# Softmax sums folded across partitions by transfers in a four-layer graph network on one Trainium2 core

## The chip, the cores and the metric

The kernel runs on one core of a Trainium2 chip. The core has a matrix engine (TensorE, PE in the profile, with its weight loads as PEld), VectorE (DVE), ScalarE (ACT), GpSimd (POOL), and a queue engine (SyncE, SP) that issues transfers; POOL issues transfers too. Matrix products are written to PSUM, which has eight banks; everything else is worked on in SBUF, with 128 partitions. The metric is the device time of one execution in microseconds; the time before is the median of three, 2737.14 us (2736.57 to 2737.26).

## The reference

Sixty-four graphs of 256 nodes with 256 features pass four layers; each layer's result is added to its input and normalized. The first is a masked attention with eight heads of 32 features and a feed-forward part, the second and third are graph attention layers, the fourth is a relational convolution in two steps. The change touches the first layer alone:

```python
qkv = x @ Wqkv.T + bqkv                       # 8 heads of 32
scores = einsum('bhqd,bhkd->bhqk', q * scale, k)
scores = where(allowed[:, None], scores, -inf)   # edge, edge back, or diagonal
attn = softmax(scores, axis=-1)
ctx = einsum('bhqk,bhkd->bhqd', attn, v)
x = layernorm(x + ctx @ Wo.T + bo, ln1_g, ln1_b)
ff = relu(x @ W1.T + b1) @ W2.T + b2
x = layernorm(x + ff, ln2_g, ln2_b)
```

## The kernel before

Each graph is recorded as a list of operations (`graph(g)`): engine, cost, what it reads and writes, and a function that issues it. A planner (`Plan.schedule`) then goes through the operations of all 64 graphs at once and writes one order for each engine. It takes operations by due date, `DUE[kind] + LATER[graph]`, two tables in the file, as soon as their inputs, their buffers (rings of a set size, `RINGS` and `SMALL`) and their engine are free by the planner's own costs; for PE it also weighs a change of tile shape against the due date (`WORTH`, `HOLD`), and `WINDOW` says how far an operation may go ahead of the earliest one that waits. So the order is written out by hand in effect, graphs overlap deeply, and a change of one operation can move all others.

Keys lie on partitions and queries along the free dimension. In `attention`, for each of two blocks of 128 keys (kt), eight scores products are made in row tiles of 32 x 128 (L969; the mode is called "row"); r counts the four heads of a row tile, hg the two halves of the heads. ACT takes the exponential (L975), DVE multiplies by the mask (L977), which gives eight tiles p of [128 keys, 2 hg, 256 queries]. DVE adds the two key blocks into four tiles `both` (L982). Then `values` issues, as one operation of PE in column tiles of 128 x 32 (mode "col"): for each half hg four products of a matrix of ones with `both` (L991), which spread the sum over 128 keys to 32 partitions for each head, and eight products of v with p (L996). Each half has a bank: sums in its second part, values in its first. DVE takes the reciprocal of the sums straight from PSUM, 128 x 256 for each half (L1002), and multiplies (L1003). ACT adds the inverse up for a check that picks a general path for unusual inputs (L1005).

`product_plus` then multiplies by Wo and adds the residual. In `feed_forward` DVE multiplies the normalized x1 by ln1_g and adds the row b2 (which was added to ln1_b in the set-up), both by `with_row` (L782). `add_row_later` and `add_later` (L787) make such an addition by a transfer instead: POOL issues a transfer that adds its source to its destination; bo, ln2_b and the residual of the last layer are added so. `masks` turns the adjacency by four PE transposes (L911) and makes the masks. `layer_norm` has statistics on DVE, the inverse root in four small POOL instructions (L887 to L890) and the scaling on ACT (L894). The full products go through `product` (L873), the gathers of the convolution are L1155. Transposed inputs of the layers go through DRAM by two SP transfers (rows, T).

Of the kernel before, what the change touches and what calls it, by code (L numbers as in the profile page):

```python
# [18 lines left out]
P = 128  # L19
# [14 lines left out]
RINGS = {"x": 3, "adj": 4, "bits": 2, "am": 2, "gm": 6, "T": 4, "qk": 2, "v": 2, "p": 12, "both": 4, "inv": 1, "ctxT": 2, "X": 8,  # L34
         "xr": 1, "hid": 1, "h": 3, "e": 3, "n": 1, "rel": 3, "hi": 2, "lo": 2, "o": 4, "blocks": 1, "turned": 1, "xT": 2, "cols": 2, "pf": 3}
DRAM = {"rows": 8, "row": 6}
SMALL = {"mv": 8, "st": 4, "rstd": 8, "r": 6, "rdeg": 4}


WORTH, HOLD, WAIT, LOCK = 20.0, 0.0, 1000000.0, -0.5  # L40
WINDOW, FIRST, TAIL = 4.0, 6, 58
LANES = 8
DUE = [
    115.11, 130.1, 87.27, 113.55, 184.78, 267.91, 127.15, 3.7, 6.4, 850.28, 907.96, 17.01, 767.99, 288.87, 535.33, 276.68, 323.52, 314.8, 295.86, 329.82,
    300.15, 372.49, 286.87, 287.98, -502.68, 591.19, 64, 190.54, 194.31, 213.9, 713.3, 602.04, 241.89, 284.25, 282.43, 286.42, 332.5, 286.53, 340.1, 391.1,
    -896.08, 82.57, 223.73, 1512.3, 652.66, -43.08, 40.01, 326.22, 390.1, 385.75, 460.35, 501.93, 1085.72, 819.32, 729.09, 1434.36, 1462.97, 1572.86, 309.27, 377.7,
    422.98, 298.61, 489.54, 349.1, 349.77, 403.91, 409.77, 1039.63, 1164.93, 1206.11, 1047.88, 1793.82, 1345.99, 941.63, 462.04, -143.68, -426.28, -563.2, -305.02, 262.4,
    -8.54, -682.53, -1425.23, -878.48, -910.48, 17.76, -1230.15, -1241.9, -450.83, -995.94, -1138.75, -609.23, -940.48, -121.13, -36.53, 517.96, -269.05, 397.54, 54.48, 413,
    377.06, 153.19, 158.68, -378.26, 790.96, -31.03, 404.99, 300.98, 1238.57, 734.43, 1000.75, 626.51, 101.96, 382.13, 45.13, 270.56, -211.2, 112.91, -26.02, 715.95,
    909.95, 879.4, 1800.2, 738.61, -248.98, -17.6, 171.18, 86.17, 653.43, -436.69, 887.7, -60.25, 1415.03, -622.37, 760.39, 726.88, -39.87, 361.21, 51.78, -354.13,  # L50
    -811.15, -996.74, -21.07, -458.08, -355, -638.8, -301.25, -345.83, 35.99, -729.94, 342.61, 978.89, 501.93, 624.52, -156.62, 34.99, -355.8, -535.26, -1056.55, -853.61,
    -309.82, -604.29, -123.96, -430.91, 250.59, -935.54, -71.5, 785.28, 299.06, 741.23, 514.78, 1612.86, 44.41, -201.89, -507.28, 48.76, -1134.8, -1513.38, -738.99, -2121.1,
    -1887.25, -2427.69, -1547.71, -1074.55, -1743.55, -801.23, -1039.08, -1445.41, -1451.37, -1811.92, -1599.65, -1352.15, -803.41, 105.4, 51.2, -2.45, 905.11, 340.42, 479.09, 446.27,
    -346.11, -241.48, -1320.8, -1184.67, 227.95, -410.93, 181.58, 411.97, 33.28, 533.62, 973.02, 416.68, 625.02, -116.64, 219.42, -238.55, -103.18, 369.86, -1126.9, -254.14,
    -62.97, -478.61, -760.52, 195.37, 133.89, -1164.69, -221.19, 309.39, -223.51, -1384.43, -912.86, -586.25, -502.37, -752.61, -194.22, -177.7, -903.8, -82.98, 212.44, 450.15,
    -20.63, 600.03, 718.67, -372.99, -463.15, -655.56, -114.2, -441.38, -98.81, -1186.92, 2.55, 33.89, -212.9, 343.42, -941.93, -141.06, 434.71, -230.33, -762.23, -500.28,
    -737.15, -1236.95, 350.32, -429.54, 392.55, 735.93, -165.46, 17.17, -406.76, -280.33, -545.61, -118.67, -562.59, -662.05, -637.17, -123.17, -299.09, -894.99, -728.14, 308.8,
    -407.46, -591.06, -1279.97, -1171.47, -1185.92, -532.14, -839.14, -1199.67, -1382.19, -1710.49, -1500.13, -823.47, -1317.15, -1651.44, -1534.52, -1542.11, -1999.83, -2099.36, -2677.74, -1674.04,
    -2031.11, -886.93, -741.03, 141.07, -201.09, -665.49, -899.61, -1034.61, -519.13, 753.8, -330.91, 224.95, -439.11, -74.6, -388.8, 150.07, 320.46, 266.34, 661.45, -131.11,
    -575.29, -614.71, -909.95, -860.38, -218.26, -502.7, 299.21, -466.82, -157.72, -96.09, 95.71, -751.12, -80.72, -711.21, -1440.05, -1626.75, -1496.54, -701.82, -2131.37, -1553.57,  # L60
    -767.95, -883.9, -451.78, -721.17, -77.66, -81.75, -876.87, -264.16, -284.81, 164.33, 500.84, 572.97, 751.67, 221.66, -573.04, -421.79, -309.92, 661.24, -78.37, 822.6,
    402.49, 814.87, 925.8, 120.82, 1121.82, 521.23, 871.11, 987.71, 661.55, 675.71, 250.34, -481.05, -752.44, -688.49, -790.45, -353.78, -477.33, -799.05, -598.48, -834.15,
    135.16, 359.04, -419.04, -153.16, -427.9, -63.74, 206.11, 144.64, -396.59, 87.54, -508.49, 33.99, 247.18, -231.56, 116.24, 559.54, 113.68, 945.19, 114.83, 632.95,
    846.63, 23.88, 241.92, -60.66, 167.66, 426.06, -250.81, -25.85, -886.96, 163.03, 213.44, 144.25, -197.06, 214.87, 469.41, 48.09, 314.49, 729.23, 840.48, 272.15,
    949.87, -274.06, 407.94, 518.88, 627.68, -253.81, -324.22, 788.98, 182.1, 73.25, -283.59, -278.9, -438.37, -351.07, -11.1, 234.91, 791.22, 267.52, -262.82, 221.58,
    -55.85, -273.21, -716.88, -232.74, -243.65, -337.37, -686.64, 243.63, -363.44, 102.34, -294.19, 157.49, -122.58, 818.8, 167.06, -139.62, 564.19, 183.5, 40.04, 561.24,
    -469.96, -301.06, 183.9, -432.22, 344.47, -19.44, 175.22, -329.23, 111.52, 31.67, 0, 12.49, 16.35, 40.7, 13.03, 29.97, 79.66, 87.72, 88.16, 92.57,
    16.9, 42.2, 63.91, 67.37, 69.2, 69.57, 64.77, 66.51, 67.73, 68.1, 54.65, 63.05, 66.15, 90.74, 93.34, 103.29, 93.94, 113.24, 100.44, 111.1,
    101.32, 106.37, 89.66, 91.55, 102.68, 90.95, 92.88, 92.14, 95.53, 92.74, 96.15, 112.62, 115.22, 115.84, 108.16, 120.58, 126.02, 128.08, 123.52, 127.74,
    128.55, 132.38, 133.45, 134.52, 135.25, 136.34, 139.84, 156.74, 162.92, 141.05, 141.83, 146.74, 158.73, 159.93, 153.03, 155.22, 160.92, 162.78, 158.68, 159.54,  # L70
    161.3, 162.04, 154.36, 156.09, 161.67, 162.41, 156.95, 157.81, 160.55, 163.15, 165.1, 168.73, 172.37, 173.1, 174.18, 178.53, 179.69, 180.41, 181.13, 184.82,
    188.33, 190.19, 190.97, 195.88, 202.19, 203.65, 203.07, 206.36, 222.82, 225.76, 209.06, 211.91, 217.09, 223.82, 225.27, 228.89, 231.63, 234.38, 242.79, 245.03,
    235.73, 243.83, 244.01, 246.19, 248.14, 251.65, 257.58, 258.36, 263.28, 272.62, 274.23, 269.16, 273.95, 276.54, 341.81, 276.37, 276.67, 281.05, 288.88, 287.58,
    292.81, 294.47, 301.47, 303.32, 303.53, 307.8, 309.41, 309.85, 304.06, 309.25, 311.17, 313.08, 313.83, 318.66, 320.01, 324.08, 327.59, 217.6, 300.09, 321.45,
    331.08, 331.85, 336.77, 350.16, 352.09, 353.9, 355.27, 348.44, 350.37, 351.98, 353.57, 356.31, 359.28, 360.19, 360.79, 357.08, 357.99, 359.21, 361.32, 361.85,
    365.25, 366.27, 367.05, 374.16, 388.51, 395.12, 397.74, 400.66, 385.92, 388.51, 398.17, 401.4, 402.41, 406.64, 404.62, 407.66, 408.19, 415.16, 418.79, 420.65,
    446.91, 460.58, 469.56, 476.66, -42.08, -71.22, 47.55, 3.95, 87.01, -47.02, 84.87, 96.85, 43.29, 49.34, 127.81, 93.06, 163.1, 82.32, 60.43, 233.39,
    93.62, 90.44, -0.5, 120.06, -23.99, 59.25, 35.15, -243.24, 80.37, 53.47, 200.92, -73.58, -7.08, 5.9, -5.15, 25.23, 43.87, 9.22, -39.39, -39.72,
    -111.42, -25.63, 15.17, 9.26, 110.12, -23.73, 207.1, 32.19, 46.32, 175.57, 73.87, -13.49, 97.45, -54.1, 63.07, 26.32, 36.13, -21.71, 254.66, 142.72,
    97.69, 92.02, 135.98, 306.53, 204.66, 18, 8.92, 47.55, 119.05, -168.79, 195.29, 2.68, 311.48, 151.91, 107.66, 214.4, 509.65, 39.08, 110.14, 228.99,  # L80
    218.6, 168.24, 162.95, 261, 207.45, 107.57, 85.27, 116.9, 164.82, 190.13, 200.94, 178.43, 163.52, 204.35, 300.87, 365.21, 103.17, 173.45, 85.86, 207.98,
    118.88, 159.89, 216.01, 206.38, 237.86, 161.11, 165.29, 97.74, 298.8, 356.49, 241.18, 307.97, 312.06, 315.69, 319.21, 317.42, 336.22, 140.04, 396.8, 241.36,
# [266 lines left out]
def tile_gnn_stack(ctx: ExitStack, tc: tile.TileContext, t: dict, out: bass.AP):  # L349
# [267 lines left out]
    def main_path(plan):  # L617
# [139 lines left out]
        def graph(g):  # L757
# [12 lines left out]
            def new(ring, shape, dtype=F32):  # L770
                return plan.tile(ring, shape, dtype)
# [702 lines left out]
```

## Time and profile before

| what | value |
| --- | --- |
| median of three runs | 2737.14 us |
| profiled execution, its own time | 2740.2 us |
| its span, first to last instruction | 2738.3 us |
| granted TensorE clock, mean | 0.995 |
| instructions | 48644 |
| DMA traffic | 329.91 MB, mean 120 GB/s |
| share of 16 DMA engines: hardware queue, software queue | 36.1%, 11.9% |
| transfers that add, issued by POOL | 64 bo, 64 ln2_b, 62 residuals, 256 KB each |
| their median time from issue to landing | 4.5, 3.8 and 4.6 us |

In a group's row, the text before the bar names the line, the engine, the operation, what it writes and reads, and how often; after the bar stand the busy time in all, the mean in ns of one, and the idle time of the engine before such instructions with what ended it. Matmuls are pipelined, and their ends are modelled, so a matmul's own duration is longer than its share of PE's time; distances from start to start tell that share. PE's fp32 matmuls have two records each. The chain of waits is followed back from the last instruction and shows, piece by piece, what held up the end.

### The profile page before, as it was taken

Reading aid. Unit: us, or ns where it says so; the run is one execution under the profiler, and the core shown is the slowest. Engines: PE = TensorE matmul, PEld = TensorE weight load, DVE = VectorE, ACT = ScalarE, POOL = GpSimd, SP = SyncE. Lnnn points to the kernel's source line nnn. Section 1 sums busy time; section 2 is a strip of 40 time slices with the busy share of each in tenths; the row PEclk is TensorE's granted clock in tenths of the full one; section 3 lists DMA queues with packets and bytes.
Section 4 is the critical chain, followed back from the end, with each engine's and each line's share of the span. In section 5 each row is a group of like instructions: output and inputs, shape, how many; then the busy total and the mean of one; then the engine's idle time right before and its main releaser. Section 6 shows DMA issues by size and latency. Waiting matters only on the chain.

```text
span 2738.3 us, 48644 instructions
## 1 busy us (share of the span) xinstructions
PE 2712.7 (99%) x15808; PEld 2115.7 (77%) x15808; DVE 2465.2 (90%) x6538; ACT 1598.4 (58%) x3830; POOL 935.5 (34%) x1747
## 2 busy tenths in 40 slices
PE   8999999999999999999999999999999999999997
PEld 6887877777787787777777877877877777778774
DVE  6789989999999999999999999999999999988977
ACT  4446555556556556556555565565565555655767
POOL 2233333334333333333333333343333333332222
PEclk8999999999999999999999999999999999999999
DMA  7345545454454454554544544544545546364211
GB/s 187 95 110 130 130 116 129 119 127 123 127 135 120 128 130 121 129 124 129 133 120 124 139 119 125 135 121 127 129 121 132 125 128 147 97 143 108 51 47 40
DMA packets 609611, 329.91 MB, mean 120 GB/s; under 512 B 391694, under 2 KB 600616, under 8 KB 609352
## 3 DMA queue, kind: packets, MB, share of 16 engines
q1 hardware_dynamic: 564984, 275.72, 36.1%
q0 software_dynamic: 44368, 51.01, 11.9%
q8 instruction: 128, 2.10, 0.3%
q14 instruction: 131, 1.07, 0.1%
HBM read 182.60 MB, written 94.23 MB: 101 GB/s over the span
## 4 chain that ended last, share of the span: by engine, by line
PE 97%; DVE 1%; DMA 1%; ACT 1%; issue 0%; SPq 0%; POOL 0%; POOLq 0%
PE bank L873 80%; PE bank L969 5%; PE bank L1155 4%; PE bank L996 4%; PE bank L991 2%; PE bank L911 1%; DMA wqkv<-in_WqkvT_dram 0%; PE bank L802 0%; DMA rows<-turned 0%; ACT turned L813 0%; DVE p L977 0%; ACT e L1170 0%; DMA T<-rows 0%; DVE inv L1002 0%; ACT X L894 0%
## 5 line engine op out<-in xcount | busy, mean ns | idle before, releaser
L887 POOL TENSOR_SCALAR rstd<-mv 128x2 f32<-128x2 f32 x384 | 148.7, 387 | 1415.1 <-DVE mv L884 469.0
L873 PE MATMUL bank<-cw,T 128*128 128x512 f32 x1024 | 469.0, 592 | 0.0
L873 PE MATMUL bank<-T,w 128*128 128x256 f32 x2048 | 466.6, 380 | 0.0
L873 PE MATMUL bank<-w,hid 128*128 128x256 f32 x2048 | 457.0, 381 | 0.0
L873 PEld LDWEIGHTS bank<-w,hid 128*128 128x128 f32 x2048 | 397.0, 196 | 43.0 <-issue 3.4
L873 PEld LDWEIGHTS bank<-T,w 128*128 128x128 f32 x2048 | 384.8, 190 | 53.8 <-issue 2.0
L975 ACT ACTIVATE p<-bank 128x512 f32<-128x512 f32 x512 | 298.8, 603 | 169.9 <-PE bank L969 169.7
L894 ACT ACTIVATE X<-X,rstd 128x256 f32<-128x256 f32 x640 | 350.0, 599 | 78.1 <-POOL rstd L890 77.3
L977 DVE TENSOR_TENSOR p<-p,am 128x512 f32<-128x512 f32 x512 | 336.6, 681 | 27.4 <-ACT p L975 22.8
L888 POOL TENSOR_TENSOR rstd<-rstd,neghalf 128x2 f32<-128x2 f32 x384 | 315.0, 820 | 32.0
L873 PEld LDWEIGHTS bank<-cw,T 128*128 128x128 f32 x1024 | 198.8, 195 | 164.5 <-issue 144.8
L1031 ACT ACTIVATE hid<-bank,col_b 128x256 f32<-128x256 f32 x512 | 212.5, 469 | 105.3 <-PE bank L873 104.1
L873 PE MATMUL bank<-h,e 128*128 128x259 f32 x1024 | 264.3, 382 | 0.0
L873 PE MATMUL bank<-gw,T 128*128 128x258 f32 x1024 | 255.1, 381 | 0.0
L873 PE MATMUL bank<-xT,wqkv 128*128 128x256 f32 x1024 | 253.7, 385 | 0.9 <-DVE xT L865 0.9
L1002 DVE RECIPROCAL inv<-bank 128x256 f32<-128x256 f32 x128 | 217.2, 1729 | 30.7 <-PE bank L996 30.5
L882 DVE BATCH_NORM_STATS2 st<-X 128x6 f32<-128x256 f32 x640 | 238.3, 414 | 2.2
L873 PEld LDWEIGHTS bank<-gw,T 128*128 128x128 f32 x1024 | 198.8, 196 | 46.3 <-issue 24.6
L873 PEld LDWEIGHTS bank<-h,e 128*128 128x128 f32 x1024 | 186.5, 190 | 46.4 <-issue 14.9
L873 PEld LDWEIGHTS bank<-xT,wqkv 128*128 128x128 f32 x1024 | 193.0, 192 | 30.6 <-issue 2.5
L1155 PE MATMUL bank<-hi,rel 128*128 128x258 f32 (+1 forms) x512 | 182.6, 364 | 0.1
L824 DVE STREAM_TRANSPOSE turned<-X 128x512 f32<-128x512 f32 x236 | 166.1, 704 | 4.6 <-ACT X L894 3.1
(147 smaller groups left out, 4676.9 us busy)
## 6 DMA issues: line engine op xcount, KB each, us to landing
rows<-turned SPq DMA_DIRECT2D x295, 256.0 KB
T<-rows SPq DMA_DIRECT2D x295, 256.0 KB
adj<-in_adj_dram SPq DMA_DIRECT2D x128, 256.0 KB
x<-in_x_dram SPq DMA_DIRECT2D x64, 256.0 KB
xr<-in_x_dram SPq DMA_DIRECT2D x64, 256.0 KB
x<-row_bo POOLq DMA_DIRECT2D x64, 256.0 KB, 4.5
xr<-row_ln_b POOLq DMA_DIRECT2D x64, 256.0 KB, 3.8
out_dram<-o SPq DMA_DIRECT2D x64, 256.0 KB
```

Of the source, the lines that this page charges most:

```text
L824: dve(0.63, lambda: nc.vector.transpose(turned().rearrange("p k (b n i) -> p (k b) i n", b=4, i=NB), xt().rearrange("p i (j c) -> p j i c" ...
L873: nc.tensor.matmul(dst, lhsT=lhs(c), rhs=rhs(c), start=(c == 0), stop=(c == n - 1))
L882: nc.vector.bn_stats(stat()[:, i, :], y()[:, i, :])
L887: nc.gpsimd.tensor_scalar(rstd()[:, 0, :], mv()[:, :, 1], 1.0, EPS, op0=ALU.mult, op1=ALU.add)
L888: nc.gpsimd.tensor_tensor(rstd()[:, 0, :], rstd()[:, 0, :], neghalf[:, 0:NB], op=ALU.pow)
L894: nc.scalar.activation(y()[:, i, :], y()[:, i, :], AF.Identity, bias=rstd()[:, 1, i : i + 1], scale=rstd()[:, 0, i : i + 1])
L969: nc.tensor.matmul(s[r]()[:, hg, :], lhsT=qk()[f, KB + hg, kt * P : (kt + 1) * P], rhs=qk()[f, hg, :], start=True, stop=True)
L975: act(0.58, lambda pr=pr, k=k, sr=s[r]: nc.scalar.activation(pr(), sr(), AF.Exp, accum_out=seen_sum[:, k : k + 1]), [s[r]], [pr])
L977: dve(0.60, lambda pr=pr, kt=kt: nc.vector.tensor_tensor(pr(), pr(), am()[:, kt, None, :].to_broadcast([P, KB, N]), op=ALU.mult), [pr, am] ...
L1002: dve(1.67, lambda hg=hg, pc=pc: nc.vector.reciprocal(inv()[:, hg, :], pc()[:, 1, :]), [pc], [(inv, hg)])
L1031: act(0.36, lambda f=f, k=k, ph=ph: nc.scalar.activation(hid()[:, f + k, :], ph()[:, k, :], AF.Relu, bias=b1[:, f + k : f + k + 1]), [ph, ...
L1155: nc.tensor.matmul(pa()[:, 0:n], lhsT=rel()[:, i, j * P : (j + 1) * P], rhs=part()[:, i, 0:n], start=(c == 0), stop=(c == len(terms) - 1))
```

## The change

The four tiles `both` become one tile of [128, 2, 4, 256]. After the four additions, two adding transfers from POOL fold it: for the first half of the heads, partitions 64 to 127 are added to 0 to 63, for the second, partitions 0 to 63 to 64 to 127. The products of ones then take 64 rows each and stand ahead of all products of values, eight in a row, in tiles of 64 x 32. The sums are transposed by DVE in blocks of 32 x 32, so that 16 columns hold all of them; the reciprocal is taken of those 16 columns, and a second transpose, which reads each column 32 times, spreads them again. The multiplication by the inverse then follows for both halves. ACT's sum reads the 16 columns. In `feed_forward`, b2 is added by a transfer. The rings change (adj from 4 to 3, pf from 3 to 2, both from 4 to 1 larger tile, inv to two tiles `sums`, a small ring `compact`), as do `WORTH`, `HOLD`, `WINDOW` and all of the tables `DUE` and `LATER`; LATER steps by 41.772 before and by 41.415 after in its middle part.

```diff
-RINGS = {"x": 3, "adj": 4, "bits": 2, "am": 2, "gm": 6, "T": 4, "qk": 2, "v": 2, "p": 12, "both": 4, "inv": 1, "ctxT": 2, "X": 8,
-         "xr": 1, "hid": 1, "h": 3, "e": 3, "n": 1, "rel": 3, "hi": 2, "lo": 2, "o": 4, "blocks": 1, "turned": 1, "xT": 2, "cols": 2, "pf": 3}
+RINGS = {"x": 3, "adj": 3, "bits": 2, "am": 2, "gm": 6, "T": 4, "qk": 2, "v": 2, "p": 12, "both": 1, "sums": 2, "ctxT": 2, "X": 8,
+         "xr": 1, "hid": 1, "h": 3, "e": 3, "n": 1, "rel": 3, "hi": 2, "lo": 2, "o": 4, "blocks": 1, "turned": 1, "xT": 2, "cols": 2, "pf": 2}
-SMALL = {"mv": 8, "st": 4, "rstd": 8, "r": 6, "rdeg": 4}
-WORTH, HOLD, WAIT, LOCK = 20.0, 0.0, 1000000.0, -0.5
-WINDOW, FIRST, TAIL = 4.0, 6, 58
+SMALL = {"compact": 3, "mv": 8, "st": 4, "rstd": 8, "r": 6, "rdeg": 4}
+WORTH, HOLD, WAIT, LOCK = 18.33, 0.32, 1000000.0, -0.5
+WINDOW, FIRST, TAIL = 17.79, 6, 58
...
-                both = [new("both", [P, KB, N]) for r in range(4)]
+                both, half = new("both", [P, KB, 4, N]), P // 2
                 for r in range(4):
-                    dve(0.60, lambda r=r: nc.vector.tensor_tensor(both[r](), p[0, r](), p[1, r](), op=ALU.add),
-                        [p[0, r], p[1, r]], [both[r]], "uses")
-                inv = new("inv", [P, KB, N])
+                    dve(0.60, lambda r=r: nc.vector.tensor_tensor(both()[:, :, r, :], p[0, r](), p[1, r](), op=ALU.add),
+                        [p[0, r], p[1, r]], [(both, r)], "uses")
+                for hg in range(KB):
+                    into, out_of = slice(half * hg, half * hg + half), slice(half - half * hg, P - half * hg)
+                    op("POOL", 1.3, lambda hg=hg, into=into, out_of=out_of: nc.gpsimd.dma_start(
+                        both()[into, hg], both()[out_of, hg], accum_op=ALU.add),
+                       [(both, r) for r in range(4)], [(both, "lo" if hg else "hi")], lag=2.4, size=0.9)
+                sums, inv, compact = new("sums", [P, KB, N]), new("sums", [P, KB, N]), new("compact", [P, KB * N // 32])
                 pcs = [new("bank", [P, 2, N]) for hg in range(KB)]
 
                 def values():
                     for hg in range(KB):
+                        rows = slice(half * hg, half * hg + half)
+                        for r in range(4):
+                            nc.tensor.matmul(pcs[hg]()[32 * r : 32 * r + 32, 1, :], lhsT=ones[rows, :], rhs=both()[rows, hg, r, :],
+                                             start=True, stop=True)
+                    for hg in range(KB):
                         pc = pcs[hg]()
-                        for r in range(4):
-                            nc.tensor.matmul(pc[32 * r : 32 * r + 32, 1, :], lhsT=ones, rhs=both[r]()[:, hg, :],
-                                             start=True, stop=True)
...
-                pe("col", 2.58, values, [v] + both + list(p.values()), pcs, [ctxT, inv])
+                pe("col", 2.15, values, [v, both] + list(p.values()), pcs, [ctxT, compact])
                 for hg in range(KB):
                     pc = pcs[hg]
-                    dve(1.67, lambda hg=hg, pc=pc: nc.vector.reciprocal(inv()[:, hg, :], pc()[:, 1, :]), [pc], [(inv, hg)])
+                    dve(0.40, lambda hg=hg, pc=pc: nc.vector.transpose(sums()[:, hg, :], pc()[:, 1, :]), [pc], [(sums, hg)])
+                dve(0.17, lambda: nc.vector.reciprocal(compact(), sums().rearrange("p k (j d) -> p (k j) d", d=32)[:, :, 0]),
+                    [sums], [compact])
+                dve(0.63, lambda: nc.vector.transpose(inv().rearrange("p k n -> p (k n)"),
+                                                      compact()[:, :, None].to_broadcast([P, KB * N // 32, 32])),
+                    [compact], [inv], "uses")
+                for hg in range(KB):
+                    pc = pcs[hg]
                     dve(0.33, lambda hg=hg, pc=pc: nc.vector.tensor_tensor(
-                        ctxT()[:, hg, :], pc()[:, 0, :], inv()[:, hg, :], op=ALU.mult), [pc, (inv, hg)], [(ctxT, hg)])
-                act(0.62, lambda: nc.scalar.activation(inv(), inv(), AF.Identity, accum_out=seen_inv[:, g : g + 1]), [inv], [inv])
+                        ctxT()[:, hg, :], pc()[:, 0, :], inv()[:, hg, :], op=ALU.mult), [pc, inv], [(ctxT, hg)])
+                act(0.3, lambda: nc.scalar.activation(compact(), compact(), AF.Identity, accum_out=seen_inv[:, g : g + 1]),
+                    [compact], [compact])
...
-                with_row(x1, b2, ALU.add, [c_b2])
+                add_row_later(x1, b2, [c_b2])
```

## The prediction

> **What bounds the kernel now.** I read the first two parts of the page, then the chain of waits, then the same chain cut to one graph of the middle, then stages. The busy times alone would allow two bounds, PE (99%) and DVE (90%):
>
> ```profile
> PE 2712.7 (99%) x15808; PEld 2115.7 (77%) x15808; DVE 2465.2 (90%) x6538; ACT 1598.4 (58%) x3830; POOL 935.5 (34%) x1747
> PE 97%; DVE 1%; DMA 1%; ACT 1%; issue 0%; SPq 0%; POOL 0%; POOLq 0%
> ```
>
> A busy PE is not yet a full PE, so the chain is cut to 987.69 to 1029.41 us, one graph. Columns: start, us, what.
>
> ```profile
> 987.69 14.88 PE bank L873 x52
> ...
> 1009.66 7.79 PE bank L873 x36
> 1017.45 0.57 PE bank L991 x8
> 1018.02 0.86 PE bank L996 x16
> 1018.88 0.43 PE bank L991 x8
> 1019.31 0.86 PE bank L996 x16
> 1020.17 0.33 PE bank L911 x4
> 1020.50 6.97 PE bank L873 x32
> 1027.47 1.94 PE bank L969 x32
> ```
>
> No other engine stands in it: the next graph's 52 products begin at 1029.41, so a graph costs 41.72 to 41.74 us of PE. Every fp32 matmul has two records. In the timeline 28 records of 256 columns run from 1009.50 to 1015.54, so a record takes 0.216 us. L991's 8 records are 4 matmuls in 0.43 us, two times 0.216: the four 32-column products of a half run together. The stages say where PE isn't full; columns: length, then PE, PEld, DVE, ACT, POOL busy (instructions), clock, DMA share, GB/s.
>
> ```profile
> 0.00:60.00 60.00, 50.44 (x358) 38.19 (x358) 37.94 (x87) 27.17 (x76) 17.15 (x29) 0.89 0.75 197
> 60.00:120.00 60.00, 58.42 (x408) 46.81 (x412) 49.90 (x97) 32.14 (x91) 14.12 (x22) 0.97 0.40 96
> 987.69:1029.41 41.72, 41.72 (x246) 32.65 (x245) 38.49 (x103) 24.45 (x60) 15.28 (x28) 1.00 0.51 128
> 2680.00:2738.30 58.30, 44.06 (x184) 26.81 (x181) 42.76 (x139) 41.65 (x79) 14.98 (x35) 0.92 0.16 42
> ```
>
> PE idles 9.6 + 1.6 us before 120 us and 14.2 us after 2680, and is full between. So 64 graphs of 41.73 us make 2670.7 of the span of 2738.3 us, and filling and draining the rest, 67.6. Only PE time per graph, or a new wait of PE, can move the result.
>
> **PE, the one term on the path.** The products of ones take 0.43 us for each half of the heads, twice: 0.86. In the changed kernel the eight have 64 rows each, one half of the heads in rows 0 to 63 and the other in 64 to 127, each half with its own bank. If all eight run together, that is 0.43 us: **0.43 saved**. That row tiles run together is seen in the scores (L969): 32 records of 32 rows take 1.94 us, where one by one they would take 32 x 0.216 = 6.9. No row has 64 x 32 tiles; row tiles and column tiles each overlap, so I take that both do together; the bound is no saving (last rival but one).
>
> Changing the tile shape costs PE time. Into 128 x 32: 0.57 - 0.43 = 0.14. Out of it, to the four transposes of the mask (L911): these last 1020.11 to 1020.34, 0.23, in the timeline, and 0.33 here: 0.10. The next full product: 6.97 - 32 x 0.216 = 0.07. Before, that is 0.31 a graph. For the row tiles: in, 1.94 - 8 x 0.216 = 0.21; out, 14.88 less 36 records of 0.216 and 16 of 512 columns at 0.43 (1032.05 to 1033.77 for four), 0.22.
>
> The order of the changed kernel in its steady part is: scores, 28 full matmuls, gathers, 2 full, gathers, 2 full, gathers, 24 full, 4 mask transposes, 8 products of ones, 16 of values, 16 full (W2), scores. The same 72 full matmuls as before; mask transposes now come ahead of the attention block. Three shape changes are left there: into 64 x 32, which I price as into 128 x 32, 0.14 (bounds 0.14 and 0.21, the row tiles); from 64 x 32 to 128 x 32, which is new and shown nowhere: bounds 0 and 0.22 (out of row tiles), taken 0.14, as the nearest row enters the same 128 x 32; out to full, 0.10 + 0.07 = 0.17 (bounds 0.10, 0.22). Sum 0.45, bounds 0.24 and 0.65. The gathers (L1155) leave no gap in the timeline, so three groups of them in place of four cost nothing.
>
> Net a graph: 0.43 - (0.45 - 0.31) = **0.29 saved**; bounds 0.50 and 0.09. Times 64: 18.6 us, bounds 32.0 and 5.8.
>
> On that inner step the Trainium skill speaks against the change: TensorEngine Tiling, "Tiling Modes", Key Properties, says that going to another tiling mode, not just another tile, drains the engine. The 0.10 to 0.22 us at each change of shape here agree, so I leave the step in; without the rule it might have been put at 0, which would make the sum 64 x 0.14 = 9.0 us lower.
>
> **DVE, beside PE.** Rows that go or give prices:
>
> ```profile
> L1002 DVE RECIPROCAL inv<-bank 128x256 f32<-128x256 f32 x128 | 217.2, 1729 | 30.7 <-PE bank L996 30.5
> L824 DVE STREAM_TRANSPOSE turned<-X 128x512 f32<-128x512 f32 x236 | 166.1, 704 | 4.6 <-ACT X L894 3.1 <-DMA rows<-turned 1.3
> L1046 DVE STREAM_TRANSPOSE cols<-h 128x64 f32<-128x64 f32 x118 | 26.7, 226 | 0.3 <-issue 0.3
> L1091 DVE RECIPROCAL r<-bank 128x1 f32<-128x1 f32 x256 | 35.5, 153 | 4.6 <-PE bank L873 4.6
> L782 DVE TENSOR_TENSOR X<-X,row_b 128x512 f32<-128x512 f32 x64 | 42.9, 671 | 0.0
> L787 POOL DMA_DIRECT2D o<-X x62 | 58.4, 942 | 227.3 <-DVE o L1171 201.1 <-DVE am L920 12.3 <-DVE hi L1148 7.4
> ```
>
> Two reciprocals of 1.73 go. Two transposes of 128x256 come: between 0.226 at 64 and 0.704 at 512 columns, 0.43 each; one reciprocal of 128x16, between 0.153 at 1 and 1.729 at 256, 0.25 (bounds 0.153 and 1.729); one transpose of 128x512, 0.70. That is 3.46 against 1.81; b2's addition takes 0.67 more away: DVE falls from 38.5 to 36.2 us a graph. It isn't on the chain, so this is worth 0 in the sum. ACT's look at the inverse shrinks from 0.63 to about 0.20 (its row of 128x1), also worth 0. What it buys is cover for the new steps; without PE in front, DVE would set the end at 36.2 us a graph.
>
> **POOL, SP and DMA.** Three adding transfers more per graph, two folds and b2's row, on POOL's queue (rows 0.94, 1.29 and 1.62 us to issue): 2.8 to 4.9 us, and POOL goes from 15.3 busy to at most 20.2 of 41.7. Behind the folds in that queue stand the four steps of the next two layer norms' roots (0.39, 0.82, 0.30, 0.34 us), then b2's row; ACT waits for the roots, which PE's products wait for later. Queue 0 takes 11.9% of the span for 190 such transfers, 1.7 us each, so three add 5.1 us: the DMA share goes from 0.51 to about 0.63. SP issues as many transfers as before but through one buffer of adj and one of pf fewer; a transfer that lands later there shows as idle time of DVE ahead of L1081 (before: 1.8 us in 236) or of PE. I price this at 0 because DVE gains 2.3 us a graph; without that cover it is as in the last rival.
>
> **The fold's wait, at nothing, and what hides it.** PE's block now waits for two transfers that start after the last of the four additions (L982). If POOL is free: two issues of at most 1.62 us, then 4.6 us to landing (o<-X), 7.8 us. In the changed order DVE has 33 instructions between that addition and its first instruction after the block, 12.7 us by their rows; 2.6 of these may fall to the block itself (1 + 4 waves of 0.43 with changes of shape), which leaves about 10.1. Slack 2.3 us. POOL itself in front: below. After the block 16 full matmuls (6.9 us) and the scores (1.9) come before Wo needs the result; DVE's chain up to it is 0.86 + 0.25 + 0.70 + 2 x 0.39 plus mask steps of 0.28 and 0.41 and an e step of 0.67: 4.0 us. So 4.9 us to spare.
>
> **Ends.** Filling and draining I leave at 67.6; one graph's latency grows by at most 7.8 - 1.6 us if the fold lies on it, which is put in the range, not in the sum.
>
> **Sum.** 2738.3 - 18.6 = 2719.7 of span. The profiled execution took 2740.2, 1.9 more than its span and 3.1 more than the median of 2737.1. So 2719.7 + 1.9 - 3.1 = **2718.5 us**; my own range is 2710 to 2730.
>
> **Rivals.**
> - *No price inside the block:* 64 x 32 to 128 x 32 is free and the others are at their low ends: 0.50 a graph, 2738.3 - 32.0 - 1.2 = 2705. For it: the eight matmuls sit in the same 32-column tiles. Against: no change of shape here is free but that to the gathers.
> - *The row halves don't overlap:* the ones take two times 0.43 as now, and the new change of shape is extra: 0.14 x 64 = 9.0 us slower, 2746. Against it: the row tiles of the scores. This is also the case that the change doesn't do what it says. It decides once the ones cost over 0.72 us.
> - *The folds land late, the other side:* if POOL starts the folds behind an ln2_b row (1.29) and a root (1.85), the second lands 7.8 + 3.1 = 10.9 us after the addition, against 10.1 of cover. PE then waits 0.8 us a graph: 2718.5 + 51 = 2770. It decides from 0.29 us of lateness a graph. For it: POOL's root rows wait long in the trace of before (469 us for mv), so its queue holds others up; against: PE sets the pace, and POOL is idle half the time.
>
> **How the numbers follow.** First case 0.64, free inside 0.15, no overlap 0.12, late folds 0.09. The range 2703 to 2741 takes in the first two but for a few hundredths and a third of the third; outside are late folds and most of the third. A change of 0.2% (5.5 us: 2731.7 to 2742.6) is what a measurement here can tell from none. Faster: 0.64 + 0.15 + 0.02 = 0.81; within: 0.08; slower: 0.11.
>
> **What would show it.** In the chain of one graph: a graph of 41.4 us; one piece of 16 records of ones of about 0.57 (0.43 with 0.14 in front), then 32 records of values of 1.73 + 0.14. If the ones last 0.86, halves don't overlap. Idle of PE before the ones, released by a transfer into both, shows the late fold. DVE's busy time should be 2317 us, POOL's 1110 to 1250. Wrong would be the whole if DMA, DVE or POOL took more than a per cent of the chain.

## The result and the profile after

The changed kernel takes 2744.83 us in the median of 11 runs (2743.12 to 2747.45), the kernel before 2737.21 in the median of 11 beside it: a ratio of 1.0028, with a 95% interval of 1.0019 to 1.0037. It is slower by 0.28%, where a gain was forecast: 2718.5 us, with a range of 2703 to 2741. The profiled execution took 2744.83 us, its span is 2743.0. The profiled execution of the kernel before took 2740.2 us, 3.0 more than its median, so the two spans lie 4.7 us apart where the medians lie 7.6 apart.

The first two parts of the page, the software queue's row and the chain of waits of the changed kernel:

```profile
PE 2706.9 (99%) x15808; PEld 2101.1 (77%) x15808; DVE 2346.9 (86%) x6602; ACT 1554.2 (57%) x3830; POOL 1086.7 (40%) x1939
...
q0 software_dynamic: 72016, 101.36, 23.0%
...
PE 91%; DVE 4%; DMA 2%; ACT 1%; issue 1%; POOL 0%; SPq 0%; POOLq 0%; DVEq 0%; ACTq 0%
```

PE's busy time fell by only 5.8 us in 64 graphs. The chain tells more: PE had 97% of it, now it has 91%, and DVE and DMA have taken the rest. Two graphs of the middle show both of its forms. First one in which nothing waits, from the chain cut to 1857 to 1902 us (start, us, what; a piece called "issue" is time in which the engine waited for nothing that the profile shows):

```profile
1857.30 0.22 PE bank L912 x4
1857.52 0.59 PE bank L997 x16
1858.12 1.86 PE bank L1004 x32
1859.98 7.11 PE bank L874 x32
...
1898.80 0.22 PE bank L912 x4
```

The block of the attention is as forecast: the 16 records of ones stand together in 0.59 us, with the change of shape in it. A graph lasts 41.50 us here. And now a graph at 1020 us, in the same view:

```profile
990.51 8.84 PE bank L874 x32
999.64 2.09 ACT X L895 x4
1002.36 0.42 DVE lo L1159
...
1011.65 0.63 DVE both L983
1012.32 0.51 issue
1012.82 0.55 POOL both L987
1013.38 7.96 DMA both<-both
1021.47 0.64 PE bank L997 x8
1022.11 1.86 PE bank L1004 x32
1023.97 7.11 PE bank L874 x32
```

PE isn't first here: between its 32 products at 990.51 and the ones the chain runs over ACT, a row of DVE instructions, POOL and a transfer. The fourth addition ends at 1012.28, the second fold lands at 1021.34, and the second half of the ones waits for it. In the next graph the same pieces return, with 7.96 us of transfer again. The page's waits of PE hold little of this (1.4 us for `both`), so it is read from the chain and from the distances between blocks.

Those distances divide the span into three stages: up to the values of the 13th block in order of time, 42 graphs, and the rest. Times in us, worked out from the traces' starts of the values; the last column counts distances over 41.6 us among the 42. The last six kernels are those of the experiments. In e1 and e13 the values open the block, in the others they stand 0.6 us behind its start; for that alone the start of these two reads 0.6 us shorter and the tail 0.6 longer.

| kernel | start | 42 graphs | tail | median graph | over 41.6 |
| --- | --- | --- | --- | --- | --- |
| before | 474.2 | 1753.8 | 510.3 | 41.73 | all, its own pace |
| after | 479.1 | 1752.5 | 511.4 | 41.51 | 15 |
| e1_ones_last | 477.3 | 1743.5 | 512.0 | 41.51 | 0 |
| e2_no_fold | 473.1 | 1743.4 | 510.2 | 41.51 | 0 |
| e8_adj_later | 479.5 | 1763.4 | 511.4 | 41.84 | 24 |
| e12_adj_slots | 477.5 | 1748.4 | 512.3 | 41.52 | 11 |
| e14_adj_after | 477.7 | 1743.7 | 511.5 | 41.51 | 1 |
| e13_first_plain | 474.6 | 1743.5 | 511.8 | 41.51 | 0 |

The PE term is there: 0.22 us in each graph that doesn't wait, 14.1 for 64. Against it the span grew by 4.7, so 18.8 us were lost: 7.5 in the start (4.9 longer in place of 2.6 shorter), 8.0 in the middle (1.3 shorter in place of 9.3), 3.3 in the tail. By the medians it is 7.6 + 14.1 = 21.7, since the traced execution of the kernel before is longer than its median. The stages by windows of the changed kernel (length, then PE, PEld, DVE, ACT, POOL busy, clock, DMA share, GB/s) put the idle time of PE at the same ends as before, with more of it:

```profile
0.00:60.00 60.00, 45.34 (x289) 35.60 (x290) 30.30 (x80) 22.82 (x66) 12.39 (x22) 0.94 0.78 186
60.00:120.00 60.00, 56.47 (x410) 42.49 (x413) 42.10 (x95) 26.51 (x76) 22.82 (x37) 0.94 0.71 142
2680.00:2743.00 63.00, 47.40 (x194) 28.75 (x193) 45.45 (x148) 43.37 (x82) 14.30 (x36) 0.90 0.14 35
```

### The profile page after: what moved, and what is told of

It reads as the page before. It is cut to its first block, busy times and chain, and to the rows that moved or that the text cites. A ratio compares the mean times of both kernels' runs of the same rounds, so it can differ in the third digit from the quotient of the medians.

```text
span 2743.0 us, 49225 instructions
## 1 busy us (share of the span) xinstructions
PE 2706.9 (99%) x15808; PEld 2101.1 (77%) x15808; DVE 2346.9 (86%) x6602; ACT 1554.2 (57%) x3830; POOL 1086.7 (40%) x1939
## 4 chain that ended last, share of the span: by engine, by line
PE 91%; DVE 4%; DMA 2%; ACT 1%; issue 1%; POOL 0%; SPq 0%; POOLq 0%; DVEq 0%; ACTq 0%
PE bank L874 76%; PE bank L970 5%; PE bank L1004 4%; PE bank L1171 4%; PE bank L997 2%; DMA both<-both 1%; DMA wqkv<-in_WqkvT_dram 1%; ACT X L895 1%; PE bank L912 0%; DVE p L978 0%; DVE o L1181 0%; DMA adj<-in_adj_dram 0%; DVE st L883 0%; PE bank L803 0%; DVE X L1126 0%
## 5 line engine op out<-in xcount | busy, mean ns | idle before, releaser
L888 POOL TENSOR_SCALAR rstd<-mv 128x2 f32<-128x2 f32 x384 | 122.1, 318 | 981.3 <-DVE mv L885 770.3
L874 PE MATMUL bank<-T,w 128*128 128x256 f32 x2048 | 472.3, 379 | 0.0
L874 PEld LDWEIGHTS bank<-w,hid 128*128 128x128 f32 x2048 | 396.1, 196 | 60.5 <-issue 10.1
L987 POOL DMA_DIRECT2D both<-both x128 | 113.3, 1015 | 357.7 <-DVE both L983 212.1
L1158 ACT CAST hi<-bank 128x256 fp32r<-128x256 f32 x256 | 94.4, 369 | 266.5 <-PE bank L874 265.8
L874 PEld LDWEIGHTS bank<-h,e 128*128 128x128 f32 x1024 | 193.1, 190 | 50.6 <-issue 22.9
```

What stands on the lines that cost most here:

```text
L874: nc.tensor.matmul(dst, lhsT=lhs(c), rhs=rhs(c), start=(c == 0), stop=(c == n - 1))
L888: nc.gpsimd.tensor_scalar(rstd()[:, 0, :], mv()[:, :, 1], 1.0, EPS, op0=ALU.mult, op1=ALU.add)
L987: op("POOL", 1.3, lambda hg=hg, into=into, out_of=out_of: nc.gpsimd.dma_start(both()[into, hg], both()[out_of, hg], accum_op=ALU.add), [(b ...
```

## The experiments

**e1_ones_last and e2_no_fold: does PE wait for the fold?** e1 puts the ones behind the values inside the block, so that 1.86 us of products hide the end of the fold; the order of everything else is that of the changed kernel.

```diff
                     for hg in range(KB):
-                        rows = slice(half * hg, half * hg + half)
-                        for r in range(4):
-                            nc.tensor.matmul(pcs[hg]()[32 * r : 32 * r + 32, 1, :], lhsT=ones[rows, :], rhs=both()[rows, hg, r, :],
-                                             start=True, stop=True)
-                    for hg in range(KB):
                         pc = pcs[hg]()
...
+                    for hg in range(KB):
+                        rows = slice(half * hg, half * hg + half)
+                        for r in range(4):
+                            nc.tensor.matmul(pcs[hg]()[32 * r : 32 * r + 32, 1, :], lhsT=ones[rows, :], rhs=both()[rows, hg, r, :],
+                                             start=True, stop=True)
```

> Same planner order as the changed kernel; inside PE's attention block the 32 records of values come first and the products of ones last, so the block no longer starts by waiting for the folds: they get 1.9 us more. Theory A, the folds land late: the waits of PE for them (some 8.5 us over graphs 23 to 41 by the periods above 41.51) go, every graph of the middle takes 41.5 us, time 2744.8 - 8 = 2735 to 2738. Rival, the new order is late by itself (DVE or POOL behind, and the fold only the last of several): graphs of 42 us stay, time 2742 to 2747.

e2 issues no fold (the sums are then those of 64 of the 128 keys) and adds 1e-6 in the addition:

```diff
-                    dve(0.60, lambda r=r: nc.vector.tensor_tensor(both()[:, :, r, :], p[0, r](), p[1, r](), op=ALU.add),
+                    dve(0.60, lambda r=r: nc.vector.scalar_tensor_tensor(both()[:, :, r, :], p[0, r](), 1e-6, p[1, r](), op0=ALU.add, op1=ALU.add),
...
-                    op("POOL", 1.3, lambda hg=hg, into=into, out_of=out_of: nc.gpsimd.dma_start(
-                        both()[into, hg], both()[out_of, hg], accum_op=ALU.add),
+                    op("POOL", 1.3, lambda: None,
```

> Leaves the two folding transfers out, so the products of ones add 64 of the 128 keys alone, and the addition ahead of them adds 1e-6 so that no sum is zero; same planner order, same tiles. Theory A: as with ones last, 2735 to 2738, no waits in the middle, graphs of 41.5 us; DMA share back from 0.63 to about 0.55. If the transfers also hold up others (SP's), the time falls below that, to 2730 to 2734. Rival: the order itself is late, 2742 to 2747.

e1 took 2734.26 us, 0.9984 [0.9974, 0.9993] of the kernel before; e2 2729.42, 0.9966 [0.9954, 0.9979]. Each lies a little below the times expected, far from those of the rival. In both the middle is 1743.4 to 1743.5 us and no graph is over 41.6: the loss of the middle is PE's wait for the fold, and 1.9 us more of cover are enough to end it. The spans of e2 and e1 differ by 6.1 us, all of it at the ends: with both marks set to the start of the block, 4.8 us in the start, where one distance between blocks fell from 24.45 to 20.05, and 1.2 in the tail. There the transfer lies bare on the path of a single graph: in the changed kernel the first two distances together are 37.6 us, in e1 37.4 and in e2 33.0, so where the ones stand in the block hardly matters there.

**e3_loads_later: is the start longer because set-up loads crowd each other?** The due dates of five loads of the graph layers' weights are moved back.

```diff
+LOADS_LATER = {37: 10.0, 38: 10.5, 63: 20.0, 61: 21.0, 65: 22.0}
+for k, at in LOADS_LATER.items():
+    DUE[k] = round(at - LATER[0], 3)
```

> The changed kernel with five set-up loads of later layers' weights (gw, cw) put behind the loads that the first graphs need. Theory B, the start is slow because these loads were put in front (PE idles 18.2 us before 120 us, 11.1 in the kernel before): the start gains 5 to 8 us, time 2737 to 2740. Rival, the start is slow because the fold lengthens the first graphs' chains: PE idles about 18 us before 120 still, time 2743 to 2747.

2748.99 us, 1.0035 [1.0021, 1.005]: not better than the changed kernel and above both times expected, and its start is 482.6 us. Putting these loads later doesn't shorten the start; nothing here speaks for their place as the cause.

**e5_before_tiles: the PE term alone.** The kernel before, in its own order, with the ones of both halves first and in 64 by 32 tiles; there is no fold, so half of the keys are left out of the sums, and the addition adds 1e-6.

```diff
+                        rows = slice(64 * hg, 64 * hg + 64)
...
-                            nc.tensor.matmul(pc[32 * r : 32 * r + 32, 1, :], lhsT=ones, rhs=both[r]()[:, hg, :],
+                            nc.tensor.matmul(pcs[hg]()[32 * r : 32 * r + 32, 1, :], lhsT=ones[rows, :], rhs=both[r]()[rows, hg, :],
                                              start=True, stop=True)
+                    for hg in range(KB):
+                        pc = pcs[hg]()
```

> The kernel before, in its own order, with the products of ones alone put into 64 x 32 tiles ahead of the values, without a fold (so they add 64 of 128 keys; the addition ahead adds 1e-6). This is the PE term alone. If 0.43 saved less 0.13 to 0.21 of changes of shape is right: 0.22 to 0.30 us a graph, 41.43 to 41.51, time 2737.2 - 14 to 19 = 2718 to 2723. If a PE that is 1% quicker runs into its producers in this order: periods of 41.6 and more, 2725 to 2737.

2721.24 us, 0.9935 [0.9919, 0.9952]. Its chain of one graph:

```profile
1010.10 0.59 PE bank L991 x16
1010.70 1.86 PE bank L998 x32
1012.56 0.33 PE bank L911 x4
1012.89 6.97 PE bank L873 x32
```

0.59 + 1.86 in place of 0.57 + 0.86 + 0.43 + 0.86: 0.27 us a graph, and the graph is 41.46 us. The tiles bring what the prediction said they bring; what takes it back isn't PE's own time.

**e6_before_turned and e7_b2_vector: the parts on DVE and b2.** e6 is the kernel before with the reciprocal taken of turned sums, for each half (`few` is a new tile of eight columns):

```diff
-                    dve(1.67, lambda hg=hg, pc=pc: nc.vector.reciprocal(inv()[:, hg, :], pc()[:, 1, :]), [pc], [(inv, hg)])
+                    def inverse(hg=hg, pc=pc):
+                        nc.vector.transpose(inv()[:, hg, :], pc()[:, 1, :])
+                        nc.vector.reciprocal(few, inv()[:, hg, :].rearrange("p (j d) -> p j d", d=32)[:, :, 0])
+                        nc.vector.transpose(inv()[:, hg, :], few[:, :, None].to_broadcast([P, N // 32, 32]))
+
+                    dve(1.67, inverse, [pc], [(inv, hg)])
```

> The kernel before, in its own order, with the turned reciprocal alone (for each half a transpose, a reciprocal of 8 columns, a transpose back: about 1.0 us in place of 1.73). Theory: DVE is not on the chain, so its 1.5 us a graph are worth nothing: 2736 to 2739, DVE busy about 100 us less. Rival, DVE paces PE through buffers: 2725 to 2733.

e7 is the changed kernel with b2 added by DVE at the place of the transfer:

```diff
-                add_row_later(x1, b2, [c_b2])
+                op("POOL", 1.3, lambda: nc.vector.tensor_tensor(x1(), x1(), b2[:, None, :].to_broadcast([P, NB, D]), op=ALU.add),
+                   [x1, c_b2], [x1], lag=2.4, size=0.9)
```

> The changed kernel with b2 added by DVE at the same place of the order, in place of the transfer. Theory C, the folds land late because they share the transfer engines with loads and turns that SP issues beside them; b2's row is issued 6 us after the folds and has no part in it: PE's waits stay, 2742 to 2747. Rival, the third adding transfer on POOL's queue makes the lateness: waits go, 2735 to 2739.

e6: 2738.61 us, 0.9998 [0.9989, 1.0008], with DVE busy for 2387.5 us in place of 2465.2. 78 us less on DVE change nothing. e7: 2744.88, 1.0025 [1.0016, 1.0035], the time of the changed kernel; b2's transfer has no part in the loss that these intervals could show.

**e8_adj_later and e12_adj_slots: is it the smaller ring of adj?** Which transfers stand beside the folds is seen in SP's queue of the changed kernel, around the fold issued at 1012.82:

```profile
1013.25 0.38 SPq L779 DMA_DIRECT2D adj<-in_adj_dram  x1
1013.72 0.42 SPq L833 DMA_DIRECT2D T<-rows  x1
1014.23 1.34 SPq L1067 DMA_DIRECT2D pf<-row  x1
```

In the 28 graphs from the 15th to the 42nd block these three are issued 0.4, 0.9 and 1.4 us after the first fold; in most of the graphs after them T comes 2 us or more before the fold and pf 3.4 after it, and no adj. Windows of both (columns as above), 8 us and 5 us from a first fold on:

```profile
1013.00:1021.00 8.00, 8.00 (x46) 6.51 (x44) 7.64 (x26) 5.25 (x12) 4.59 (x8) 1.00 0.86 196
1848.00:1853.00 5.00, 5.00 (x24) 4.37 (x24) 4.94 (x16) 4.29 (x8) 4.17 (x7) 1.00 0.71 125
```

DVE reads an older adj at 1012.80 (rel<-adj), and 0.4 us later SP issues the load of adj, with T and pf behind it in its queue: it looks as if that load waits for the buffer, since adj's ring was cut from four to three. e8 moves adj's due date:

```diff
+DUE[482] += 22.0
```

> The changed kernel with the load of the mask's adj due 22 us later, so that SP does not issue it between the two folds (in the waiting graph at 1013.25, the folds at 1012.82 and 1013.38). Theory C: the second fold lands 5.5 to 6.5 us after its issue in place of 8.0, most of PE's waits go, 2735 to 2739. Rival, the folds take 7 to 8 us by themselves: 2742 to 2747. Other SP transfers may take adj's place beside the folds; then landing stays over 7 us and the theory is not decided.

2754.39 us, 1.0052 [1.0035, 1.0068], slower than either side expected. SP then issued T 0.3 us before the fold, pf 0.5 and adj 0.9 after: adj had changed places but not left. The folds were later still. That decided nothing about the ring. e12 freezes the order and gives adj a fourth buffer, taken in the order of use; the room comes from the second transpose, which now writes the inverse back into the tile `sums` that held the sums (those lines aren't shown):

```diff
-        for o in plan.schedule():
+        done, seen = plan.schedule(), {"adj": [], "sums": []}
+        for o in done:
+            for u in o.tiles:
+                if u.ring in seen and u not in seen[u.ring]:
+                    seen[u.ring].append(u)
+        begin = {id(u): min(o.start for o in done if u in o.tiles) for u in seen["adj"]}
+        held = [None] * 4
+        for u in sorted(seen["adj"], key=lambda u: begin[id(u)]):
+            u.slot = min((0.0 if x is None else x.end, i) for i, x in enumerate(held) if x is None or x.end <= begin[id(u)])[1]
+            held[u.slot] = u
+        for u in seen["sums"]:
+            u.slot = 0
+        for o in done:
             o.issue()
```

> The changed kernel in its own order, with four buffers of adj in place of three (the room comes from spreading the inverse back into the tile that held the sums). If a load of adj that waits on SP for its buffer holds T and pf back until they run beside the folds: SP issues the three earlier, the folds land in 5 to 6 us throughout, PE no longer waits in graphs 23 to 41, the excess over 41.51 us a graph falls from 9.3 to under 3, and the time is 2734 to 2739. If the folds land late for a cause that adj's buffers have no part in (their own length beside whatever runs, POOL's start): 2742 to 2747, with 10 or more graphs over 41.6 us as now.

2739.61 us, 1.0005 [0.9995, 1.0014]. Neither theory's whole account: SP issued the three 0.9 us earlier, the middle became 4.1 us shorter, but 11 graphs were still over 41.6 and the folds not shorter. The time lies between the two expectations. So the ring has a part, through the moment at which SP issues, and the transfers are still beside the folds.

**e14_adj_after: the transfers beside the fold.** The order is that of the changed kernel, adj has three buffers, and only the loads of adj near a fold go seven SP transfers back, behind the blocks.

```diff
-        for o in plan.schedule():
+        done = plan.schedule()
+        queue = [o for o in done if o.engine == "SP"]
+        folds = [o.start for o in done if o.engine == "POOL" and any(u.ring == "both" for u in o.tiles)]
+        for o in [o for o in queue if any(u.ring == "adj" for u in o.tiles) and 12 < o.graph < 50]:
+            if any(-1.5 < o.start - at < 4.0 for at in folds):
+                behind = queue[queue.index(o) + 7]
+                done.remove(o)
+                done.insert(done.index(behind) + 1, o)
+        for o in done:
```

> The changed kernel, with every load of adj that SP issues within 1.5 us before to 4 us after a fold issued seven SP transfers later, behind the four loads of blocks; nothing else moves, and adj keeps three buffers. If the folds are late because SP's transfers share the 16 DMA engines with them: 256 KB fewer beside them at 196 GB/s are 1.3 us, the folds of graphs 14 to 41 land in 5.5 to 7 us after their issue in place of 6.6 to 8.1, the excess over 41.51 us a graph falls from 9.3 to under 3, and the time is 2736 to 2739.5. If the folds need 7 to 8 us by themselves (their own packets, their start on POOL): excess of 6 or more and 2742 to 2747.

2735.66 us, 0.999 [0.9981, 0.9999]; 9.2 us less than the changed kernel, by the place of one 256 KB load a graph, and just under the time expected. SP's queue beside the fold that e14 issues at 1009.2:

```profile
1008.83 0.36 SPq L833 DMA_DIRECT2D T<-rows  x1
1009.62 0.34 SPq L1067 DMA_DIRECT2D pf<-row  x1
1013.57 0.36 SPq L828 DMA_DIRECT2D rows<-turned  x1
1014.76 1.93 SPq L863 DMA_DIRECT2D blocks<-in_x_dram  x4
1016.73 0.46 SPq L779 DMA_DIRECT2D adj<-in_adj_dram  x1
```

PE's chain is back at 97%, and the middle at 1743.7 us:

```profile
PE 97%; DVE 1%; DMA 1%; ACT 1%; POOL 0%; SPq 0%; issue 0%; POOLq 0%
```

From the first fold's issue to the last packet of the second, in the 28 graphs (from the traces' packets):

| kernel | median | least to most | graphs over 41.6 us |
| --- | --- | --- | --- |
| after | 7.3 | 6.6 to 8.1 | 15 |
| e8_adj_later | 7.6 | 6.5 to 9.2 | 24 |
| e12_adj_slots | 7.2 | 6.2 to 8.3 | 11 |
| e14_adj_after | 6.3 | 5.6 to 7.5 | 1 |
| after, the 44th to 54th | 5.8 | 5.6 to 6.5 | 0 |

With adj gone from the front of the queue, T and pf are issued earlier too, 0.3 us before the first fold and 0.5 after it in place of 0.9 and 1.4 after. That isn't what helps: in e8 they stand at the same two places, with adj behind them at 0.9, and the folds take 7.6 us there and 6.3 in e14. The load of adj is what differs between these two.

The Trainium skill says of this (DMA: Bandwidth & Descriptors, "Issuing engines are not separate DMA queues") that transfers begun by different engines run on the same 16 DMA engines and interleave. The 1.0 us between after and e14 agrees: a load on SP's queue delays an adding transfer on POOL's.

**e9_before_folded: the fold in the order of before.** Each of the four tiles is folded by itself as soon as it is added, in eight transfers of a quarter of the size, and the ones come last:

```diff
+                    def add_and_fold(r=r):
+                        nc.vector.tensor_tensor(both[r](), p[0, r](), p[1, r](), op=ALU.add)
+                        for hg in range(KB):
+                            into, out_of = slice(64 * hg, 64 * hg + 64), slice(64 - 64 * hg, P - 64 * hg)
+                            nc.gpsimd.dma_start(both[r]()[into, hg], both[r]()[out_of, hg], accum_op=ALU.add)
```

> The kernel before, in its own order, with each of the four sums tiles folded by two small transfers (64 KB) right after its addition, the values first and the products of ones last in 64 x 32 tiles; reciprocal and b2 as before. If the 0.27 us a graph of the tiles alone (2721 measured without a fold) survives, because each fold has at least 5.3 + 1.9 us before PE needs it: 2720 to 2727. If the eight issues a graph hold up the norms on POOL, or the last folds land over 7.2 us after their addition: graphs above 41.6 us, 2730 to 2760.

2812.32 us, 1.0266 [1.0249, 1.0283], far above both times expected. The groups of POOL and PE that touch `both`, in e9:

```profile
L986 POOL DMA_DIRECT2D both<-both x512 | 520.9, 1513 | 423.2 <-PE bank L1164 268.0 <-PE bank L873 55.3 <-issue 51.9
...
L1005 PE MATMUL bank<-both,ones 64*32 64x256 f32 x1024 | 76.6, 404 | 33.9 <-DMA both<-both 33.0 <-DVE n L1121 0.5
```

Issuing 512 transfers holds POOL for 520.9 us, against 113.3 for the 128 of the changed kernel. A transfer of a quarter of the size isn't cheaper to issue (1513 ns in the mean, 1015 there), and PE waited 33.0 us for the folds. Of the 75 us by which its span is longer than that of the kernel before, about 35 lie in the start, 11 in the 42 graphs and 29 in the tail. As a way to fold earlier it failed.

**e11_ends_plain and e13_first_plain: the ends.** Both are e1 with no fold and products of ones over all 128 rows in some graphs; the order stays, POOL's step issues nothing there, and the sums are whole everywhere.

```diff
+                plain = g < 9 or g >= 57
...
-                    op("POOL", 1.3, lambda hg=hg, into=into, out_of=out_of: nc.gpsimd.dma_start(
+                    op("POOL", 1.3, lambda hg=hg, into=into, out_of=out_of: None if plain else nc.gpsimd.dma_start(
...
                         for r in range(4):
+                            if plain:
+                                rows = slice(0, P)
```

> e1_ones_last with plain products of ones over all 128 rows, and no fold, in the first nine and the last seven graphs; the order of all the rest is kept, and the result is the whole one. If the time that remains above the version without a fold (2734.26 against 2729.42) is the fold's latency in the graphs that fill and drain the pipeline: graphs 2 to 6 start earlier by 4 us in all, the tail is 1 to 2 us shorter, and the time is 2727 to 2731. If the start is longer for another reason (the loads, the order of the set-up): 2733 to 2736, as e1.

2732.82 us, 0.9982 [0.9973, 0.9992]: hardly better than e1, and between the two times expected. The blocks of the start came up to 4.3 us earlier (the third one), but 16 plain graphs cost 0.27 us each, and that term I had left out of the expectation. So e13 takes `plain = g < 3`:

> e11_ends_plain with the plain products in the first three graphs alone. In e11 the blocks of the first graphs began up to 3.9 us earlier than in e1_ones_last, but each of its 16 plain graphs took 0.27 us more (periods 41.23 for 40.96 and the like), 4.3 us together. If that is the whole account: a span of 2732.9 - 3.7 + 3 x 0.27 = 2730.0 and a time of 2730 to 2732.5. If the fold's latency in graphs 3 to 8 counts as well: 2733 to 2735.

2732.19 us, 0.9979 [0.997, 0.9988], with a span of 2729.8. The span is as worked out; the fastest kernel here that computes the reference, by 5.5 us against before, and within the intervals not to be told from e11.

## Why the prediction was wrong, step by step

- *What bounds the kernel.* Right for the kernel before. For the changed one it left a point out: a late fold is not made up later. The pieces of the stalled chain go from PE's products over ACT and DVE to the additions and the fold, so the next additions are late with PE. The sign that was named for being wrong, more than a per cent of the chain on another engine, is there: 4% on DVE, 2% on DMA.
- *The PE term: right in mechanism, too large by a quarter.* The eight matmuls run together, the changes of shape cost about what was said: 0.16 into 64 by 32 (0.59 less 2 x 0.216, forecast 0.14), 0.13 from there to 128 by 32 (1.86 less 8 x 0.216, forecast 0.14), 0.20 out (7.11 less 32 x 0.216, forecast 0.17). That is 0.49 for 0.45. The graph gained 0.22 and not 0.29; the other 0.03 are spread over pieces that I can't separate. 14.1 us, not 18.6.
- *DVE worth 0.* Right, by e6. Its rows hit the prices (0.427, 0.241 and 0.698 us for 0.43, 0.25 and 0.70); its busy time is 2346.9 where 2317 was forecast. b2's addition on DVE, priced at 0.67 us a graph, is 28.0 us in e7, 0.44 a graph, for the reason of the point after the next.
- *POOL, SP and DMA worth 0.* POOL's 1086.7 us and the software queue's 23.0% are a little below what was said, and b2 is free (e7). But that 0 hid a price: one buffer of adj fewer, which I looked for in DVE's and PE's waits for that transfer, moved SP's issues next to the folds, and this costs about 5 us (e12).
- *"The fold's wait, at nothing": the step that failed.* It set 7.8 us from the last addition to the landing against 10.1 of cover. The need was right where the loads keep away: in e14 0.55 to the issue and 6.3 to the last packet. Beside adj, T and pf it is 0.55 + 7.3, and in the graph shown the second fold lands 9.06 after the addition. The cover was wrong: in the 28 graphs the ones stand 8.17 us behind the addition, not 10.1. I had summed 12.7 us of DVE's records for the distance to DVE's next step; the same stretch sums to 12.85 us here and lasts 10.90, since records overlap. In DVE's timeline of the changed kernel (start, us) each next one starts before the one ahead of it ends:

```profile
1011.59 0.69 DVE L983 TENSOR_TENSOR both<-p 128x512 f32<-128x512 f32 x1
1012.19 0.68 DVE L1100 SCALAR_TENSOR_TENSOR e<-e 128x512 f32<-128x512 f32 x1
1012.80 0.42 DVE L1141 TENSOR_SCALAR rel<-adj 128x512 fp32r<-128x512 int32 x1
```

  0.69 of record, 0.60 of time. The Trainium skill says why (Perfetto Trace Analysis, "Optimizing Scalar/DVE Operations"): the profile shows about twice an instruction's fixed overhead, since the half in which the write is acknowledged overlaps with the next instruction. The rows above show an overlap, 0.09 us of it. With 8.17 in place of 10.1 the slack would have been 0.4 us and not 2.3, and the contention of the stretch, 86% of the DMA engines, would have had to be looked at. The 10.1 would have held in the 44th to 54th graph: there DVE has 36 or more instructions in the stretch (34 in most of the 28 graphs), the ones stand 10.65 us behind the addition in the median, the last packet comes 6.3 us behind it, and no graph is late.
- *The ends at no cost.* Wrong as well. They had 10.8 of the 18.8 us. Of these the fold's latency is about 6 (e1 against e2: 4.8 in the start, 1.2 in the tail). The rest isn't settled. The changed order costs something even without a fold: the span of e2 is 6.1 us longer than that of e5, which has the same tiles in the order of the kernel before, 2.6 in the start, 0.9 in the 42 graphs and 2.6 in the tail; no run tells which of the changed tables, rings or steps does that. And e6, whose order is that of the kernel before, has a start of 470.9 us beside 474.2, so single executions differ there by 3 us without any cause that was tried.
- *The account by medians.* Between 2718.5 and 2744.83 lie 26.3 us: 4.5 for the PE term, 10.6 that e1 takes away by hiding the end of the fold, 4.8 more that go with the fold itself (e1 to e2), and 6.4 that stay without any fold. These are differences of medians of separate series, and the intervals above reach 2.5 to 3.5 us to each side.
- *The rivals.* "The folds land late" was the outcome, at a chance of 0.09 and for a reason that isn't the one it gave. POOL starts the folds 0.55 us after the addition in the median graph, the transfers themselves are slow, and 15 graphs are late by 0.2 to 1.0 us rather than all by 0.8, so that 2770 was too much. "The row halves don't overlap" and "no price inside the block" fall with 0.59 and 1.86.

## What to carry to other kernels

The cover of a new wait is a distance between starts, taken from a timeline; a sum of durations overstates it wherever the records of an engine overlap. Before such a wait is priced at nothing, look at what else moves on the DMA engines in that very stretch, in each regime of the order, and at the graphs that fill and drain the pipeline, where a latency that the middle hides can lie bare. And where a result can be consumed last in a block, as the ones can here, that may cost nothing: in e1 the graph stayed at 41.51 us and the waits of the middle went.

## What the runs showed of the hardware

- An adding transfer of 256 KB within SBUF landed 3.4 to 8.1 us after its issue in one and the same kernel, 5.2 in the median; the quickest have few other transfers beside them. One load of 256 KB more or less beside two of them is worth 1.0 us (the changed kernel against e14) to 1.3 (e8 against e14).
- Eight matmuls of 64 rows in 64 by 32 tiles, two records each, take 0.59 us with the change of shape: both row halves and all four column tiles run at once. In the trace the first eight records start within 0.05 us of each other, and so do the second eight, 0.24 us later. Going on from there to 128 by 32, in the same columns, costs 0.13 us, as much as entering that shape from full products in the kernel before (0.14).
